# W2 as seven block products, a split last group and a written-out order, in a four-layer graph kernel on one core

## The chip, the cores and the metric

The kernel runs on one core of one Trainium2 chip. The metric is the device time of one execution in microseconds, the median of several runs; lower is better. The engines are named as the profile names them: PE is TensorE (PEld its weight loads), DVE is VectorE, ACT is ScalarE, POOL is GpSimd, SP is SyncE, which here only issues DMAs.

## The reference, cut to what matters

128 graphs of 64 nodes with 256 features pass four layers. After each, the input is added and the sum is normalized over the features. Everything is float32.

```python
# layer 0: five steps of message passing with a GRU
for l in range(5):
    m = h @ weight[l]
    agg = einsum('bij,bid->bjd', A, m)
    h = gru_cell(agg, h, w_ih, w_hh, b_ih, b_hh)
x = layernorm(x + h * nodemask[..., None])
# layer 1: W1 is 256 x 1024, W2 is 1024 x 256
agg = epsilon * x + einsum('bnm,bmd->bnd', adj, x)
h = silu(rmsnorm(agg @ W1 + b1, rms_weight))
x = layernorm(x + h @ W2 + b2)
# layer 2: logmap0, aggregation over adj, expmap0, projection on a ball
x = layernorm(x + project(expmap0(adj @ logmap0(x))))
# layer 3: attention, e_i and f_j from h = x @ W_w.T + W_b
a = adj * exp(e_i + f_j + a_b);  a = a / sum(a)
x = layernorm(x + a @ h)
```

The logarithm in layer 2 is artanh(n)/n. For small n the kernel takes a power series instead of the quotient, and picks by comparing n with `SERIES_BELOW`.

## The kernel before, in words

Two graphs make a block of 128 rows; four blocks make a group of 512 rows (`NB = 4`, `R = 512`, `HR = 256`). There are 16 groups, and `group(g)` writes down all operations of one. Each group is a stream; up to four streams are in work at a time. Buffers are named slots: most tags (`U`, `V`, `agg`, `A`, `B`, `y`, `h`) exist once or twice for each of three slot sets (`s = g % 3`), so a group takes the slots of the group three before it. PSUM has eight banks, handed out one by one.

The GRU (`gated`, called five times) multiplies weights of 256 rows by activations of 256 rows as a two-by-two block product with seven products in place of eight (`gate`, L817, for the two gates; `prod`, L823, for the new state). Sums of activation blocks come from VectorE (`sums`, by way of `summing`, L354); sums of weight blocks are made once (`sums_of`, L445). W1 is done in the same way (`by_sums`, L1000). W2 is plain in the kernel before: for each half h of a group, two blocks of 128 rows, each the sum of eight matmuls with 256 columns, accumulated in a bank `ps_o1` (L316 is the helper line `matmul`). `onto_rows` (L707) then adds the bank to the residual `xb` on VectorE, and for all groups but the last two lets the same instruction give the row sums (`accum_out`) for the normalization.

`layer_norm` takes the mean from these row sums and the variance from a ScalarE square with accumulation (L725); the last two groups use VectorE's statistics instead (L733, L734). Powers of -0.5 and the like are GpSimd instructions (L737). Small scalars per row (`tiny`) have a small tile each. In layer 2 the small arithmetic runs on GpSimd for most groups (`few`, `few_s`), on VectorE for the last two. Layer 3 takes the attention weight `wattP`, whose rows are permuted to fit the transposed x3 that a DMA delivers; the last two groups transpose on TensorE (`feats_of`, L668) and use `wattT`. ScalarE's functions lie in several tables; changing from one to another is a table load. The clock of TensorE is granted by a throttle, and is shown in the profile.

The order of the operations on each engine is not that of the code. `Plan.advance` simulates engines with given durations and, in stretches of 7 us, ranks the ready operations in one of four ways, which the string `CHOICES` picks for each stretch. `Flow.issue` emits the operations in the resulting order and adds dependencies that pin the order on each engine. Some operations have two possible engines (`either`, `copied`, `scaled`), and the plan chooses.

The seven products in `gate` and `by_sums` use the scheme whose weight sums are set up like this, before any group:

```python
for o, x0, x1, op in ((ms1, ms4, mn22, OP.add), (ms3, m11, ms4, OP.subtract), (ms2, ms1, m11, OP.subtract), (ms4, m12, ms2, OP.subtract)):
    dve(512, lambda o=o, x0=x0, x1=x1, op=op: nc.vector.tensor_tensor(
        w1f[:, o, :], w1f[:, x0, :], w1f[:, x1, :], op), [(w1f, o)], [(w1f, x0), (w1f, x1)])
```

Of the kernel before, what the change touches and what calls it, by code (L numbers as in the profile page):

```python
# [22 lines left out]
SERIES_BELOW = 0.25  # L23
# [19 lines left out]
class Op:  # L43
    __slots__ = ("eng", "us", "run", "ways", "stream", "n", "kb", "sets", "need", "then", "bufs", "opens", "id", "way", "port")

    def __init__(self, ways, stream, n, kb, sets, port=()):
        self.port = port
        self.ways = {eng: (us, run) for eng, us, run in ways}
        self.eng, self.us, self.run = ways[0]
        self.stream, self.n, self.kb, self.sets = stream, n, kb, sets  # L50
        self.need, self.then, self.bufs, self.opens, self.id, self.way = 0, [], (), None, 0, 0.0


class Plan:


    def __init__(self, flow):
        self.flow = flow
        ops = [o for s in flow.streams for o in s]
        self.need = [o.need for o in ops]  # L60
        self.at = [0.0] * len(ops)
        self.uses = {}
        self.clock = dict.fromkeys(flow.AHEAD, 2.5)
        self.queues = [{e: deque(o for o in s if e in o.ways) for e in self.clock} for s in flow.streams]
        self.banks = [0.0] * BANKS
        self.left, self.first, self.bus = len(ops), 0, 0.0
        self.lands = [0.0] * flow.TRANSFERS
        self.order, self.table, self.port = [], None, 0.0

    def advance(self, until, rank):  # L70


        flow, need, at, clock, banks = self.flow, self.need, self.at, self.clock, self.banks
        while self.left and clock["PE"] < until:
            best = None
            for s in range(self.first, min(self.first + flow.WINDOW, len(self.queues))):
                for e, q in self.queues[s].items():
                    opened = False
                    for _, o in zip(range(flow.AHEAD[e]), q):
                        t = max(clock[e], at[o.id], self.port) if e in o.port else max(clock[e], at[o.id])  # L80
                        if o.opens is not None:
                            if opened or not banks or need[o.id]:
                                opened = True
                                continue
                            t = max(t, banks[0])
                        elif need[o.id]:
                            continue
                        elif o.kb and e != "POOL":
                            t = max(t, self.lands[0])
                        elif o.sets and self.table not in o.sets:  # L90
                            t += flow.TABLE
                        key = (t + flow.SOONER if len(o.ways) > 1 and e == "DVE" else t, *rank(s, o))
                        if best is None or key < best[0]:
                            best = key, o, e, t
            if best is None:
                return False
            _, o, eng, t = best
            if o.sets and self.table not in o.sets:
                self.table = o.sets[0]
            for e in o.ways:  # L100
                self.queues[o.stream][e].remove(o)
            self.order.append((eng, o))
            end = t + o.ways[eng][0]
            clock[eng] = end
            if eng in o.port:
                self.port = end
            if o.opens is not None:
                banks.pop(0)
            for b in o.bufs:
                n = self.uses.get(b, b.left) - 1  # L110
                self.uses[b] = n
                if not n:
                    banks.append(end + flow.hop(eng, "PE"))
                    banks.sort()
            if o.kb:
                self.bus = max(self.bus, end + flow.DMA[0]) + o.kb / flow.DMA[1]
                end = self.bus + flow.DMA[2]
                if o.eng != "POOL":
                    self.lands = [*self.lands[1:], end]
            for u in o.then:  # L120
                need[u.id] -= 1
                at[u.id] = max(at[u.id], end + flow.hop(eng, u.eng))
            self.left -= 1
            while self.first < len(self.queues) and not any(self.queues[self.first].values()):
                self.first += 1
        return True


class Flow:

    AHEAD = {"PE": 32, "DVE": 10, "ACT": 10, "POOL": 4, "SP": 2}


    HOPS = {"from PE": 0.22, "to PE": 0.42, "else": 0.06, "own": 0.0}

    REACH = {"from PE": 0.22, "to PE": 0.15, "else": 0.06, "own": 0.0}

    SOONER = 0.4


    DMA = (2.0, 330.0, 1.0)
    TRANSFERS = 8
# [89 lines left out]
def kernel(  # L242
# [392 lines left out]
    def group(g):  # L635
# [76 lines left out]
        def layer_norm(y, st, tag, name, norm=None):  # L712
# [6 lines left out]
            def row(b):  # L719
                return [(y, b)]  # L720
# [529 lines left out]
```

## Time and profile before

| What | Value |
|---|---|
| median of 3 runs | 2296.64 us (2296.31 to 2298.32) |
| the profiled execution, its own time | 2296.92 us |
| its span, first to last instruction | 2295.1 us |
| mean granted TensorE clock | 0.994 of full speed |
| instructions | 32440 |
| busy: PE, DVE, ACT, POOL | 2245.7, 1696.8, 1308.8, 554.3 us |

The page gives busy time by engine, then the span in 40 slices, DMA queues, the chain of work that ended last and the costliest groups of instructions. In a group's line the part after the bar is the group's busy time and the mean duration of one instruction, then the idle time of the engine just before them and what ended it. A matmul of float32 data shows as two records of the same shape, each with a weight load. Matmuls are pipelined, so that their durations overlap; how fast they follow one another is read from their starts in the timeline. The stretches (windows) give the same busy times for chosen parts of the span.

### The profile page before, as it was taken

The numbers are of one execution on the slowest core, as the hardware profiler recorded it, in microseconds if no ns is written. First come the engines' busy times: TensorE is split into PE (matmuls) and PEld (weight loads), VectorE is DVE, ScalarE is ACT, GpSimd is POOL, SyncE is SP. The second block draws the span as 40 slices with busy tenths as digits, with TensorE's granted clock in tenths as the row PEclk, the third lists the DMA queues.
The fourth block names the chain that finished last, engine by engine and source line by source line (L and its number), as shares of the span: only waits on it lengthen the run. The fifth ranks groups of instructions, "written<-read, shape, count | busy, mean of one in ns | idle before, by whom it ended". The sixth has DMA issues, their size and how long they took to land.

```text
span 2295.1 us, 32440 instructions
## 1 busy us (share of the span) xinstructions
PE 2245.7 (98%) x11242; PEld 1979.1 (86%) x11242; DVE 1696.8 (74%) x3633; ACT 1308.8 (57%) x2800; POOL 554.3 (24%) x902
## 2 busy tenths in 40 slices
PE   9999999999999999999999999999999999999986
PEld 7888888888888888888888888888888888888774
DVE  5777867767777778677777777778777777777776
ACT  3344656675556556566566656556565665555564
POOL 2200222441122223132322223222231322112201
PEclk9999999999999999999999999999999999999998
DMA  5111112121212012121211212012122121211200
GB/s 146 33 23 33 28 19 58 19 49 29 48 28 47 22 28 58 19 45 33 36 42 25 52 28 47 21 29 49 28 49 37 22 53 21 49 19 20 46 10 19
DMA packets 428771, 84.21 MB, mean 37 GB/s; under 512 B 399124, under 2 KB 427824, under 8 KB 428608
## 3 DMA queue, kind: packets, MB, share of 16 engines
q1 hardware_dynamic: 426880, 80.26, 17.7%
q8 instruction: 89, 1.46, 0.3%
q10 hardware_dynamic: 1328, 1.31, 0.2%
q0 software_dynamic: 400, 0.57, 0.1%
q14 instruction: 74, 0.61, 0.1%
HBM read 32.55 MB, written 8.39 MB: 18 GB/s over the span
## 4 chain that ended last, share of the span: by engine, by line
PE 93%; DVE 3%; ACT 1%; POOL 1%; DMA 1%; issue 1%; SPq 0%; POOLq 0%; ACTq 0%; DVEq 0%
PE p_ga L817 23%; PE p_gc L817 12%; PE ps_o L316 9%; PE ps_agg L316 7%; PE p_ix L823 6%; PE p_gb L817 6%; PE p_hx L823 6%; PE p_ah L1000 4%; PE p_hy L823 4%; PE p_iy L823 4%; PE ps_a L316 2%; PE p_ch L1000 2%; PE ps_att L316 1%; PE ps_sup L316 1%; PE p_bh L1000 1%; PE ps_wmih L316 1%
## 5 line engine op out<-in xcount | busy, mean ns | idle before, releaser
L316 PE MATMUL ps_o<-w2s,hid 128*128 128x256 f32 x1024 | 230.9, 379 | 4.3 <-ACT hid L1051 4.3
L316 PEld LDWEIGHTS ps_o<-w2s,hid 128*128 128x128 f32 x1024 | 194.0, 190 | 31.7 <-ACT hid L1051 5.5
L351 POOL TENSOR_SCALAR mv<-st 128x4 f32<-128x4 f32 x56 | 15.6, 278 | 829.5 <-DVE y L707 442.0
L339 ACT ACTIVATE hnb<-p_hx,half_b 128x256 f32<-128x256 f32 x213 | 100.3, 471 | 143.0 <-PE p_hx L823 111.7
L817 PE MATMUL p_gc<-tA,w_h 128*128 128x256 f32 x640 | 173.2, 381 | 0.1
L817 PE MATMUL p_gc<-tB,w_a 128*128 128x256 f32 x640 | 172.3, 379 | 1.1 <-DVE tB L354 1.0
L817 PE MATMUL p_ga<-tA,w_h 128*128 128x256 f32 x640 | 171.7, 379 | 0.0
L817 PE MATMUL p_ga<-tB,w_a 128*128 128x256 f32 x640 | 168.4, 379 | 1.1 <-DVE tB L354 1.1
L817 PE MATMUL p_ga<-hT,w_h 128*128 128x256 f32 x640 | 168.3, 380 | 0.7 <-DVE U L867 0.4
L817 PE MATMUL p_ga<-agg,w_a 128*128 128x256 f32 x640 | 167.1, 379 | 0.0
L316 PEld LDWEIGHTS ps_agg<-edge,hr 128*128 128x128 f32 x1024 | 142.2, 193 | 12.4 <-DVE a_t L621 3.0
L316 PE MATMUL ps_agg<-edge,hr 128*128 128x128 f32 x1024 | 143.5, 276 | 2.8 <-DVE a_t L621 2.6
L870 ACT ACTIVATE U<-U,half_b 128x512 f32<-128x512 f32 (+1 forms) x160 | 94.0, 628 | 79.7 <-DVE U L867 79.6
L817 PEld LDWEIGHTS p_gc<-tB,w_a 128*128 128x128 f32 x640 | 121.0, 190 | 17.8 <-DVE tB L354 1.6
L817 PEld LDWEIGHTS p_ga<-tB,w_a 128*128 128x128 f32 x640 | 120.5, 190 | 18.1 <-DVE tB L354 1.8
L817 PEld LDWEIGHTS p_gc<-tA,w_h 128*128 128x128 f32 x640 | 121.2, 191 | 16.6 <-ACT V L334 0.5
L817 PEld LDWEIGHTS p_ga<-agg,w_a 128*128 128x128 f32 x640 | 119.7, 190 | 15.7 <-issue 0.5
L817 PEld LDWEIGHTS p_ga<-hT,w_h 128*128 128x128 f32 x640 | 118.5, 190 | 16.0 <-DVE U L867 0.8
L817 PEld LDWEIGHTS p_ga<-tA,w_h 128*128 128x128 f32 x640 | 117.9, 190 | 14.1
L334 ACT COPY agg<-ps_agg 128x512 f32<-128x512 f32 x140 | 81.0, 579 | 78.9 <-PE ps_agg L316 77.9
L870 ACT ACTIVATE V<-V,half_b 128x256 f32<-128x256 f32 (+1 forms) x160 | 87.8, 586 | 59.5 <-DVE V L867 58.9
L883 DVE TENSOR_TENSOR V<-p_ix,V 128x256 f32<-128x256 f32 x192 | 80.6, 420 | 35.3 <-PE p_ix L823 32.4
(285 smaller groups left out, 5667.1 us busy)
## 6 DMA issues: line engine op xcount, KB each, us to landing
hr<-t SPq DMA_DIRECT2D x256, 128.0 KB, 3.2
x<-in_x_dram SPq DMA_DIRECT2D x64, 128.0 KB, 2.7
xr<-in_x_dram SPq DMA_DIRECT2D x16, 512.0 KB, 4.3
out_dram<-x_n SPq DMA_DIRECT2D x16, 512.0 KB, 2.9
xs<-in_x_dram SPq DMA_DIRECT2D x120, 64.0 KB, 2.4
x3T<-t SPq DMA_DIRECT2D x56, 128.0 KB, 3.1
edge<-in_adj_dram SPq DMA_DIRECT2D x64, 32.0 KB, 2.2
wm<-in_L_gnn_weight_dram SPq DMA_DIRECT2D x5, 256.0 KB, 3.3
```

Of the source, the lines that this page charges most:

```text
L316: return nc.tensor.matmul(o, lhsT, rhs, start=(k == 0), stop=(k == nk - 1))
L334: flow.either([("ACT", 0.22 + 0.00077 * n, lambda: nc.scalar.copy(o(), i())), ("DVE", 0.145 + 0.00105 * n, lambda: nc.vector.tensor_copy(o ...
L339: flow.either([("ACT", 0.3 + 0.0008 * n, lambda: nc.scalar.activation(o(), i(), AF.Identity, bias=bias(), scale=scale())), ("DVE", 0.145 + ...
L351: pool(0.25, lambda: nc.gpsimd.tensor_scalar(w[0](), x(), s0, s1, op0, *((op1,) if op1 else ())), [w[1]], r)
L817: pe(HR, lambda i=i, w=w, c=c: nc.tensor.matmul(ps[:, c * HR:(c + 1) * HR], w[:, m, c * P:(c + 1) * P], v[i][0](), start=first and i == 1 ...
L823: pe(HR, lambda: nc.tensor.matmul(ps[:, j * HR:(j + 1) * HR], w[:, m, :], v[0](), start=first, stop=True, skip_group_check=True), [ps], [( ...
L870: act(HR if len(w) == 1 else R, lambda: nc.scalar.activation(o(), src(), AF.Tanh, bias=half_b[:, i * KD + c:i * KD + c + 1], scale=0.5), w ...
L883: dve(HR + 44, lambda: nc.vector.tensor_add(uu[:, c, half(n)], region(ps, j), uu[:, c, half(n)]), [(uu, (n, c))], [ps, (uu, (n, c))])
L1000: pe(HR, lambda c=c: nc.tensor.matmul(ps[:, c * HR:(c + 1) * HR], w1f[:, w, (2 * q + c) * P:(2 * q + c + 1) * P], v[0](), start=first and ...
```

## The change

1. W2 is held as seven blocks of 512 x 128 (`w2f`), four of them loaded and four combinations made on GpSimd (`w2_less`), in place of the plain `w2s`. In groups 0 to 14, `by_sums_back` multiplies the hidden activations by W2 as a two-by-two block product with seven products of eight matmuls, each with 128 columns. VectorE makes eight sums of activation blocks of 128x512 (`sums`) and seven additions from PSUM to the residual (`onto`). Two banks are held, `p_ox` and `p_oy`. The row sums come from an additional ScalarE pass in `layer_norm`.
2. Group 15 keeps plain sums for W2, as matmuls of 128 columns. To get the missing block back, one combination is undone.
3. Group 15's layers 2 and 3 are two streams of two blocks each. They take slot sets of their own, load ScalarE's tables ahead of use (`table`), and in the second piece put small transposes of no use to the output on TensorE (`busy`).
4. The order is no longer planned: each step of the emission is a mark in the string `ORDER`, which names the stream, engine and place in that engine's waiting list (`placed`).
5. The series of layer 2 has three terms fewer, with `SERIES_BELOW` at 0.125 in place of 0.25. The small scalars share one tile for each slot set (`FEW`). The plain attention weight lives in a work slot at the start and is brought back by DMA for the last two groups (`att_plain`). Silu takes the hidden chunks in the order 0, 1, 4, 5, 2, 3, 6, 7.

```diff
-SERIES_BELOW = 0.25
+SERIES_BELOW = 0.125
...
-class Plan:
...
+    def placed(self):
+        at, n = self.SIGNS.index, len(self.SIGNS)
+        waiting = [{e: [o for o in s if e in o.ways] for e in self.ENGINES} for s in self.streams]
+        first, marks = 0, iter(self.ORDER)
+        for c in marks:
+            i = at(next(marks)) * n + at(next(marks)) if c == "~" else at(c)
+            i, e = divmod(i, len(self.ENGINES))
+            i, s = divmod(i, self.AHEAD)
+            o, eng = waiting[first + s][self.ENGINES[e]][i], self.ENGINES[e]
...
-    w2s = fixed([P, KH, D], "w2s")
...
+    w2f = fixed([P, 7, KQ, P], "w2f")
...
+    for o, k, n in ((w11, 0, 0), (w21, 1, 0), (w22, 1, 1), (wd3, 0, 1)):
+        flow.op("SP", 0.6, lambda o=o, k=k, n=n: nc.sync.dma_start(w2f[:, o], w2k[k, n]), [(w2f, o)], kb=256)
+    for o, x0, x1 in ((wd1, wd3, w11), (wd2, w22, wd1), (wd3, w22, wd3), (wd4, w21, wd2)):
+        w2_less(o, x0, x1)
+    wattT = unit("A", S, "wattT", (P, KD, D + 2))
...
+            if summed and of:
+                for b in range(NB):
+                    act(400, lambda b=b: nc.scalar.activation(
+                        o[:, b, :], y[:, b, :], AF.Identity, accum_out=st[:, b, 0:1]), [(o, b), (st, (0, b))], row(b))
...
+                def sums(q):
+                    for o, x0, x1, op in ((s1, a21, a22, OP.add), (s2, s1, a11, OP.subtract), (a21, a11, a21, OP.subtract), (s4, a12, s2, OP.subtract)):
+                        summing(R, lambda o=o: val(o[q]), lambda x0=x0: val(x0[q]), lambda x1=x1: val(x1[q]), op,
+                                o[q][1], [*x0[q][1], *x1[q][1]])
...
+                prod(px, 0, w11, a11, True)
+                prod(py, 0, w21, a12, True)
+                onto(0, 0, px, 0)
+                prod(py, 1, wd3, a21)
+                onto(0, 0, py, 0)
+                prod(px, 0, wd2, s2)
+                onto(1, 1, py, 1)
+                onto(1, 0, px, 0)
+                prod(py, 1, wd4, a22)
+                prod(px, 0, wd1, s1)
+                onto(1, 0, py, 1)
+                onto(1, 1, px, 0)
+                prod(px, 0, w22, s4)
+                onto(0, 1, px, 0)
...
+            if g == NG - 1:
+                w2_less(wd3, w22, wd3)
...
+        def busy(after, n=6):
+            if piece and base:
+                ps = bank("ps_warm")
...
     for g in range(NG):
         flow.stream()
-        group(g)
+        made = group(g)
+        for i in range(2 if made else 0):
+            flow.stream()
+            group(g, ((g + 1 - i) % NF, SIZES[g] // 2, SIZES[g] // 2 * i, *made))
```

## The prediction

> **What bounds the kernel now.** I read the page first: TensorE is busy for 98% of the span and carries 93% of the chain that ended last. The question is therefore how long its list of matmuls is, and where it stands idle.
>
> ```profile
> PE 2245.7 (98%) x11242; PEld 1979.1 (86%) x11242; DVE 1696.8 (74%) x3633; ACT 1308.8 (57%) x2800; POOL 554.3 (24%) x902
> PE 93%; DVE 3%; ACT 1%; POOL 1%; DMA 1%; issue 1%; SPq 0%; POOLq 0%; ACTq 0%; DVEq 0%
> ```
>
> Second, the stretches (columns: us, then busy us and instructions of PE, PEld, DVE, ACT and POOL, granted clock, DMA share, GB/s).
>
> ```profile
> 1000.00:1500.00 500.00, 499.48 (x2529) 443.97 (x2528) 374.33 (x792) 302.51 (x649) 128.79 (x202) 1.00 0.19 38
> 1500.00:2000.00 500.00, 499.39 (x2518) 443.25 (x2518) 375.91 (x802) 294.05 (x649) 135.33 (x231) 1.00 0.19 38
> 2150.00:2200.00 50.00, 41.39 (x197) 35.12 (x194) 39.04 (x96) 24.20 (x51) 5.25 (x7) 0.93 0.13 33
> 2200.00:2250.00 50.00, 45.92 (x220) 39.76 (x221) 33.48 (x75) 27.50 (x45) 6.95 (x5) 0.97 0.00 1
> 2250.00:2270.00 20.00, 8.44 (x29) 5.93 (x28) 14.66 (x71) 12.32 (x35) 4.62 (x4) 0.83 0.00 0
> 2270.00:2296.00 26.00, 14.12 (x62) 11.17 (x61) 16.02 (x60) 13.08 (x31) 3.87 (x3) 0.76 0.12 40
> ```
>
> In the middle TensorE lacks 1.1 us of 1000, and VectorE is at 75%. Of its 49.4 us idle in all (2295.1 - 2245.7), some 36 lie after 2150, at a lower clock besides. Third, the timeline of TensorE gives the true price of a matmul; the mean durations (379 ns) overlap, so starts are compared.
>
> ```profile
> 1015.61 0.59 PE L823 MATMUL p_hx<-tA,w_hn 128*128 128x256 f32 x2
> 1016.04 0.59 PE L823 MATMUL p_hy<-tA,w_hn 128*128 128x256 f32 x2
> 1016.48 1.05 PE L316 MATMUL ps_agg<-edge,hr 128*128 128x128 f32 x8
> 1017.37 0.38 PE L678 MATMUL ps_hr<-ident,hT 128*128 128x128 f32 x2
> ```
>
> A matmul with 256 columns appears as two records, 0.432 us from start to start (1015.61 to 1016.04 to 1016.48), 0.216 a record. With 128 columns and fresh weights each time, eight records take 0.89 us: 0.111 each, 0.2225 a matmul. So half the width costs 1.03 of half the time. Last, the groups and the chain at the end.
>
> ```profile
> L316 PE MATMUL ps_o<-w2s,hid 128*128 128x256 f32 x1024 | 230.9, 379 | 4.3 <-ACT hid L1051 4.3
> L707 DVE SCALAR_TENSOR_TENSOR xb<-ps_o,xb 128x256 f32<-128x256 f32 x64 | 24.9, 420 | 27.6 <-PE ps_o L316 27.6
> L357 POOL TENSOR_TENSOR sqt<-sqt,sqh 128x512 f32<-128x512 f32 x56 | 73.0, 1304 | 127.2 <-ACT sqh L986 124.0
> ```
>
> ```profile
> 2230.05 22.03 PE ps_o L316 x102
> 2252.11 0.76 DVE xb L707 x2
> ...
> 2254.28 1.65 POOL rstd L737
> ```
>
> The W2 of groups 14 and 15 is the last dense work; from 2252.1 to 2295.1, 43.0 us, both groups go through layers 2 and 3 side by side.
>
> **What the Trainium skill says.** "TensorE: Matmul & The Clock Gate", section "Wait — 56ns, not 53.3ns?", gives N / 2.4 GHz plus 2.5 ns for a warm matmul. A record here passes its columns twice by its price: 512 / 2.4 + 2.5 = 215.8 ns and 256 / 2.4 + 2.5 = 109.2; the trace has 216 and 111, so narrow matmuls are nearly free of overhead. The same page, "What's actually happening", has the clock halve after an idle window of some 3.4 us; the trace agrees, with granted clocks of 0.83 and 0.76 in the last two stretches. "SBUF — State Buffer", section "Who interferes with whom", lets a VectorE instruction with two SBUF inputs exclude a GpSimd one that reads SBUF: all eight new sums per group are of that kind. In this trace POOL's sqt sums stretch from a median of 1274 ns to at most 1761, which fits and doesn't prove it.
>
> **The change, part by part.**
>
> *W2 in seven products, groups 0 to 14.* Removed per group: 64 records of 256 columns, 64 x 0.2158 = 13.81 us. Added: 7 products of 8 matmuls, 112 records of 128 columns, 112 x 0.1112 = 12.45. Fifteen times 1.36 is 20.3. Group 15 stays plain but narrow: 128 x 0.1112 = 14.23, 0.4 worse. Net -19.9 us. Bounds for the narrow price, as no run of over 16 narrow records is shown: the skill's 109.2 ns (1808 records: -23.6), and 125, midway to the 140 that the group of ps_agg gives by its busy time (143.5 / 1024, the tails of short runs in it): +5.0. I take 111.2, since that spacing was measured with a weight load for every record.
>
> *What feeds them.* VectorE per group: 8 sums of 128x512 from SBUF, 0.70 each (L354 shows 0.69 to 0.75), 5.6; 7 adds from PSUM of 256 elements, 0.42 (L883), 2.9; gone are 4 adds with accumulator, 4 x (0.42 + 0.08) = 2.0. So +6.5 us, and the instruction list moves some 1.5 more of copies and scalings from ScalarE to it. ScalarE: 4 passes for the row sums, 0.50 + 0.19 each, +2.8. A group takes 138 us (W2 starts at 810.3 and 948.2), so VectorE goes from 75 to about 80%, ScalarE from 60 to 61%. I cost this at nothing: other groups' gates lie on TensorE meanwhile. Without that cover a group would expose the 5.6 of sums ahead of the products, and four waits in p_ox (each product after the first needs its bank read, 0.42 or 0.84 plus about 0.3 of hops): 8 to 9 us. Behind the sums on VectorE stand the gates' adds from PSUM, for which TensorE waits; the trace has VectorE at 80% and more in single stretches with TensorE full, so I allow +2 over all, bounds 0 and +10.
>
> *Setup and small steps.* Four weight loads of 256 KB for two of 512, four POOL subtractions at about 1.3 (the sqt row, same size). W2 is first wanted at 292 us, but the subtractions stand on POOL ahead of the sums for layer 1's weights (w_a), which group 0's gates want; the table of waits has POOL idle 39.1 us there for ScalarE's w_a, so their 5.2 fit. If the loads, put on SP among the other weights, come late, w_a waits with them: a few us once. The plain attention weight now comes by four DMAs of 64 KB in group 13, on SP ahead of nothing that is due for 100 us; its place in slot A is returned before group 2 wants it, or costs some us once. The shorter series drops 6 POOL operations of 0.29 in 14 groups (24 us of an engine at 24%: nothing now) and 3 of 0.17 on VectorE for each chain at the end.
>
> *The end.* After the last W2 matmul I follow the list for two-block pieces with the durations of the rows at the end of before. Adds, statistics, power: 3.2 us, but VectorE is in the first piece's scalar chain till 5.3; second piece's chain, 14 x 0.17, 7.7; scaling, aggregation, two squares, 10.1; power, tanh, two ball chains of 6 x 0.18, 14.0; y and statistics 16.1; power, offset, two scalings 18.5; transposes and copies 20; attention of the one piece and of the other, 24.5; final sums, statistics, two queued powers and the last scaling 30.8; store 4.4. About 35 against 43.0, bounds 31 and 40. What is late next is the other piece's attention, and group 14's last normalization, which is put behind both. The 24 filling transposes cost nothing where TensorE is idle; they hold the clock, which cost some 5 us here (20.5 busy for 15.6 of work at 0.216).
> TensorE's work after the last W2 shrinks from 15.6 to 13.9 (group 14's aggregation goes ahead of it): that 1.7 is added to the time before.
>
> *The order.* Groups 14 and 15 no longer do W2 together: between group 15's W1 and W2 only group 14's aggregation (1.7) covers a chain of copy 0.6, two squares 1.4, sum 0.7, row sums 0.8, power 1.3, ps_rms 0.6, VectorE 0.74, Silu 0.7 and 0.6 of hops, 7.4 in all: some 5.7 idle where before lost about 3.5, +2.2. Against this stand the waits that TensorE has now (table of waits: us in total, times, longest):
>
> ```profile
> PE p_hy L823 <- DVE y L707: 3.7, 1, 3.7
> PE p_ah L1000 <- ACT hid L334: 3.0, 3, 1.4
> PE p_ah L1000 <- DVE hid L1005: 2.7, 1, 2.7
> ```
>
> With 1.2 (ps_hr behind y L707) and 4.3 (ps_o behind hid, in the groups above) they are 14.9. An order set one operation at a time can put other products there; I take half, -7.5, bounds 0 and -14. With the +2 of VectorE: about -3.3, bounds -14 and +8.
>
> Sum on the profiled execution: span 2295.1 - 19.9 + 1.7 - 8.0 - 3.3 = 2265.6; I keep 1.4 in hand for the reordered start and call it 2267. With the 1.8 around the span that is 2268.7 against 2296.92, and the median stood 0.3 lower: 2268.
>
> **Rivals.**
> 1. *The end doesn't shorten.* Group 15's pieces share VectorE, and one's chain delays the other's; the cover lost ahead of W2 is not regained. For it: by my list some 14 of the end's first 20 us are VectorE or its waits for POOL. Then 2296.6 - 19.9 + 1.7 - 1 = 2277.
> 2. *The order removes nearly all avoidable waits.* Pre-tail idle falls by 14 and the end to 31: 2296.6 - 19.9 + 1.7 - 12 - 14 = 2252. Against it: VectorE has less slack than before.
> 3. *VectorE takes TensorE's place in W2.* p_ox is a chain of four products with a VectorE read between; if neighbouring gates wait in VectorE's queue behind the 5.6 of sums, every group stalls. Full exposure, 8.5 x 15 = 127 less the 28 above, gives about 2395; the side turns at (19.9 + 8) / 15 = 1.9 us per group. Half a group's sums exposed, 2.8: 2311. Against it: 1.1 us idle in 1000 with VectorE at 75%, and up to three other groups' products in the list between.
> That the change doesn't do what it says is excluded for W2: the instruction list has the 840 and 64 narrow matmuls.
>
> **How the numbers follow.** Forecast 0.62, rival 1 0.19, rival 2 0.14, rival 3 0.05. The range 2254 to 2281 takes the forecast's bounds and rival 1, and leaves out most of rivals 2 and 3. A difference under 0.2% (4.6 us) can't be told from no change: faster 0.95, within 0.02, slower 0.03.
>
> **What would show it.** p_ox and p_oy together 1680 records, spaced 0.111; TensorE's busy time near 2222; VectorE near 1810; idle in 1000 to 2000 still under 5; from the last ps_o to the end about 35, with a clock nearer 0.9. Spacing of 0.12 or more, or waits of p_ox on VectorE above 2 us a group, would prove me wrong.

## The result, and the profile after

| | Before | After | Forecast |
|---|---|---|---|
| median of 5 runs each, us | 2296.64 (2296.31 to 2298.45) | 2289.12 (2286.62 to 2291.02) | 2268 (2254 to 2281) |
| profiled execution, its own time / span, us | 2296.92 / 2295.1 | 2286.62 / 2284.8 | 2268.7 / 2267 |
| busy PE, us | 2245.7 | 2237.4 | near 2222 |
| busy DVE, us | 1696.8 | 1827.1 | near 1810 |
| TensorE idle, 1000 to 2000 us | 1.1 | 8.6 | under 5 |
| last matmul of W2 to the end, us | 43.0 | 36.0 | about 35 |

The ratio is 0.9963, 95% interval [0.9949, 0.9978]: faster, clear of the scatter, but by 7.5 us where 28.6 were forecast. The time lies 8 us above the upper end of the range. The profiled execution is the fastest of the five; the accounts by trace below are of it, and its span is 10.3 us shorter than that of before.

The page of after, busy time and the chain that ended last by engine:

```profile
PE 2237.4 (98%) x12050; PEld 1982.7 (87%) x12050; DVE 1827.1 (80%) x3832; ACT 1307.4 (57%) x2856; POOL 536.7 (23%) x827
PE 89%; DVE 6%; DMA 1%; ACT 1%; SPq 1%; issue 1%; POOL 0%; ACTq 0%; DVEq 0%; POOLq 0%
```

TensorE has 808 records more and is busy for less time. VectorE is at 80%, as forecast. But VectorE's share of the chain of work that ended last has gone from 3% to 6%, and TensorE's from 93% to 89%: the way back from the end now leads through VectorE more often.

The stretches of after (us, then busy us and instructions of PE, PEld, DVE, ACT and POOL, granted clock, DMA share, GB/s):

```profile
1000.00:1500.00 500.00, 494.90 (x2671) 441.91 (x2670) 407.16 (x833) 300.43 (x656) 124.45 (x187) 1.00 0.21 37
1500.00:2000.00 500.00, 496.50 (x2707) 444.14 (x2706) 410.96 (x837) 296.43 (x669) 127.95 (x208) 1.00 0.22 37
2150.00:2200.00 50.00, 45.17 (x268) 39.19 (x267) 44.84 (x86) 31.16 (x65) 12.35 (x20) 1.00 0.19 33
2200.00:2250.00 50.00, 41.66 (x252) 36.34 (x251) 37.13 (x115) 34.45 (x73) 10.68 (x11) 0.93 0.03 11
2250.00:2270.00 20.00, 15.78 (x72) 11.85 (x72) 16.79 (x84) 12.69 (x40) 4.13 (x5) 0.91 0.00 0
2270.00:2285.00 15.00, 4.19 (x17) 2.53 (x16) 8.08 (x36) 5.87 (x14) 2.40 (x3) 0.76 0.21 71
```

In the middle TensorE is idle for 5.1 and 3.5 us of 500 each, where before had 0.5 and 0.6. That is where the forecast is most clearly missed. The end, from the last matmul of W2, looks as it said: 36 us in place of 43 at a higher clock. In the order before, after:

```profile
2252.10:2295.10 43.00, 20.49 (x80) 15.62 (x80) 28.96 (x121) 24.02 (x63) 8.49 (x7) 0.79 0.07 25
2248.80:2284.80 36.00, 21.02 (x98) 15.18 (x96) 25.83 (x121) 19.73 (x55) 6.53 (x8) 0.86 0.09 30
```

The groups of W2 in after:

```profile
L1173 PE MATMUL p_oy<-w2f,hid 128*128 128x128 f32 x720 | 98.2, 275 | 1.3 <-DVE hid L434 1.1
L1173 PE MATMUL p_ox<-w2f,s 128*128 128x128 f32 x720 | 98.0, 275 | 0.5 <-DVE s L434 0.3
L1173 PE MATMUL p_ox<-w2f,hid 128*128 128x128 f32 x240 | 35.2, 275 | 0.0
L1182 DVE TENSOR_TENSOR xb<-p_ox,xb 128x256 f32<-128x256 f32 x60 | 25.2, 420 | 9.8 <-PE p_ox L1173 8.7
L396 PE MATMUL ps_o<-w2f,hid 128*128 128x128 f32 x128 | 17.1, 302 | 1.6 <-ACT hid L1149 1.6
```

The new products are all there (1680 records), and TensorE stood idle just before them for 1.8 us in the whole program. W2 itself runs as it was meant to. What is lost must lie ahead of other work.

To find it I took every matmul's distance to the start of the next one, less its price (0.216 us for 256 columns, 0.111 for 128, what undisturbed records of the traces take), and summed what is left by stretch. This is waiting and slow clock together, and it counts waits too short to be seen as idle time:

| Stretch, us | Before | After | After with GpSimd's sums in quarters (below) |
|---|---|---|---|
| 0 to 400 | 9.3 | 7.6 | 8.7 |
| 400 to 600 | 3.5 | 10.4 | 10.7 |
| 600 to 1000 | 2.5 | 1.3 | 2.5 |
| 1000 to 2000 | 2.2 | 13.5 | 4.4 |
| 2000 to 2150 | 1.9 | 0.6 | 0.7 |
| 2150 to the last matmul | 36.1 | 29.5 | 28.1 |
| sum | 55.4 | 63.1 | 55.0 |
| price of all matmuls | 2225.9 | 2208.8 | 2208.8 |

The price falls by 17.1 us: 19.8 from W2, less 2.7 for the 24 filling transposes. The waits rise by 7.7. The difference is the 10.3 us of the span, with under 1 us from what follows the last matmul. A change of the narrow price by 0.4 ns moves the two sums of after by 1.5 us against each other, and the middle stretch by 0.6.

**What stands in the way at 1017 us.** The timeline of after, four lines of it (start us, us, engine, line, operation; in brackets the idle time before it and what ended it):

```profile
1014.08 0.68 DVE L1040 SCALAR_TENSOR_TENSOR hT<-hT,V 128x512 f32<-128x512 f32 x1
...
1017.49 2.61 POOL L437 TENSOR_TENSOR x_n<-x_n,wb_r 128x1024 f32<-128x1024 f32 x1 [8.16 <-DVE t L1355]
...
1017.92 2.73 DVE L1040 SCALAR_TENSOR_TENSOR hT<-hT,V 128x512 f32<-128x512 f32 x1
...
1020.80 0.63 PE L771 MATMUL ps_hr<-ident,hT 128*128 128x128 f32 x4 [0.87 <-DVE hT L1040]
```

The same VectorE instruction takes 0.68 us at 1014.08 and 2.73 at 1017.92. The second starts 0.43 us after a GpSimd sum of two operands, which ends at 1020.10, and it ends 0.55 us after that. It did next to nothing while GpSimd ran. Then TensorE waits for its result. The Trainium skill ("SBUF — State Buffer", section "Who interferes with whom") says that a VectorE instruction with two SBUF inputs contends with a GpSimd instruction that reads SBUF, because its second input comes through an interface that both share, and "Issue order, not op shape, decides who blocks"; these four lines agree, with 2.73 us for 0.68. Below, and in the expectations, "the port" is this shared interface.

In after, 52 VectorE instructions take over 0.15 us more than is usual for their kind, 46.1 us in all (before: 36, and 28.4 us). 24.1 us of it lie beside GpSimd's `sqt` sums, 9.5 beside this `x_n` sum of 128x1024 and 9.4 beside `xb<-x_n,b_r`. These sums aren't new: before has them too.

That this is a block and not a general slowdown shows in how the 52 end. 49 of them begin while a GpSimd operation runs and end at a fixed distance behind its end: 0.55 us for two inputs of 128x512 (26), 0.28 to 0.29 for two inputs of 128x256 (14) and for a comparison of 128x512 with one input (`edge`, 5), 0.02 for 128x2 (4). So two SBUF inputs aren't the only case. 112 VectorE additions that take one operand from PSUM begin during GpSimd sums too, and none of them is longer than usual by more than 0.01 us. GpSimd's powers, mostly of 128x4 and some 1.04 us each, don't block either, an exception that the skill's rule doesn't make: 40 VectorE instructions with two SBUF inputs begin during one, and none is longer by more than 0.02 us.

What TensorE waits for in the middle of after, 1000 to 2000 us (us in total, times, longest; before has three waits there, 1.2 us in all):

```profile
PE ps_att L396 <- DVE y L800: 2.0, 2, 1.1
PE p_bh L1098 <- DVE aggm L415: 1.0, 1, 1.0
PE p_ga L915 <- DVE U L965: 0.9, 1, 0.9
PE ps_hr L771 <- DVE hT L1040: 0.9, 1, 0.9
PE p_hx L921 <- DVE hnb L420: 0.7, 1, 0.7
PE p_ga L915 <- DVE tB L434: 0.6, 1, 0.6
```

The six longest are all for VectorE and make 6.1 of the 8.6 us. Six of the seven waits in these lines end within 1.5 us of the end of a stretched VectorE instruction; the exception is `p_hx`. `ps_att` and `p_bh` follow instructions held up by the `xb` sum, `ps_hr` and `p_ga` others held up by `x_n` and `sqt`.

### The profile page after: what moved, and what is told of

The parts are those of the page before. It is cut to its first block, busy times and chain, and to the rows that moved or that the text cites. A ratio compares the mean times of both kernels' runs of the same rounds, so it can differ in the third digit from the quotient of the medians.

```text
span 2284.8 us, 34210 instructions
## 1 busy us (share of the span) xinstructions
PE 2237.4 (98%) x12050; PEld 1982.7 (87%) x12050; DVE 1827.1 (80%) x3832; ACT 1307.4 (57%) x2856; POOL 536.7 (23%) x827
## 3 DMA queue, kind: packets, MB, share of 16 engines
q1 hardware_dynamic: 428144, 80.52, 19.9%
## 4 chain that ended last, share of the span: by engine, by line
PE 89%; DVE 6%; DMA 1%; ACT 1%; SPq 1%; issue 1%; POOL 0%; ACTq 0%; DVEq 0%; POOLq 0%
PE p_ga L915 23%; PE p_gc L915 11%; PE ps_agg L396 7%; PE p_ix L921 6%; PE p_gb L915 6%; PE p_hx L921 6%; PE p_iy L921 5%; PE p_ox L1173 4%; PE p_hy L921 4%; PE p_ah L1098 4%; PE p_oy L1173 3%; PE ps_a L396 2%; PE p_ch L1098 2%; PE ps_sup L396 1%; PE ps_att L396 1%; PE p_bh L1098 1%
## 5 line engine op out<-in xcount | busy, mean ns | idle before, releaser
L915 PE MATMUL p_ga<-hT,w_h 128*128 128x256 f32 x640 | 177.4, 380 | 0.9 <-DVE U L965 0.9
L419 ACT ACTIVATE hnb<-p_hx,half_b 128x256 f32<-128x256 f32 x202 | 95.1, 472 | 105.7 <-PE p_hx L921 82.5
L396 PE MATMUL ps_agg<-edge,hr 128*128 128x128 f32 x1024 | 150.6, 276 | 4.3 <-DMA hr<-t 2.8
L915 PEld LDWEIGHTS p_ga<-tB,w_a 128*128 128x128 f32 x640 | 120.1, 190 | 16.9 <-DVE tB L434 1.3
L915 PEld LDWEIGHTS p_gc<-tB,w_a 128*128 128x128 f32 x640 | 119.7, 190 | 16.9 <-DVE tB L434 1.2
L915 PEld LDWEIGHTS p_ga<-tA,w_h 128*128 128x128 f32 x640 | 117.5, 190 | 14.2
L834 POOL TENSOR_TENSOR rstd<-ve,pow 128x4 f32<-128x4 f32 (+2 forms) x67 | 80.2, 1197 | 136.2 <-DVE ve L832 124.8
L822 ACT ACTIVATE x_n<-y,mv 128x256 f32<-128x256 f32 x168 | 83.4, 499 | 38.4 <-POOL mv L431 38.4
```

The lines of the kernel that those rows point to most:

```text
L396: return nc.tensor.matmul(o, lhsT, rhs, start=(k == 0), stop=(k == nk - 1))
L419: flow.either([("ACT", 0.3 + 0.0008 * n, lambda: nc.scalar.activation(o(), i(), AF.Identity, bias=bias(), scale=scale())), ("DVE", 0.145 + ...
L822: act(400, lambda b=b: nc.scalar.activation(o[:, b, :], y[:, at + b, :], AF.Square, bias=mv[:, b, 0:1], accum_out=st[:, b, 1:2]), [(o, b), ...
L834: pool(1.25, lambda: nc.gpsimd.tensor_tensor(rstd[:, :m, :], ve[:, :m, :], pow2[:, :m, :NB], OP.pow), [rstd], [ve])
L915: pe(HR, lambda i=i, w=w, c=c: nc.tensor.matmul(ps[:, c * HR:(c + 1) * HR], w[:, m, c * P:(c + 1) * P], v[i][0](), start=first and i == 1 ...
```

## The experiments

All ratios are against the kernel before, on the same chip. Theories go by letters in the expectations: A, the first, is that the new sums load VectorE too heavily; D, formed after the first four runs, is that GpSimd's sums block VectorE. What another theory holds is said where it is tested.

**1. The new sums cut to one column.**

```diff
-   summing(R, lambda o=o: val(o[q]), lambda x0=x0: val(x0[q]), ...
+   summing(R, lambda o=o: val(o[q])[:, :, :1], lambda x0=x0: val(x0[q])[:, :, :1], ...
```

> The changed kernel, but each of VectorE's eight sums per group ahead of the seven products works on one column of 256 instead of all, and the three products that take a sum of their own tile take the identity instead (part of W2's product is left out; the matmuls keep number, shape and order). Theory A, VectorE's new load is what TensorE waits for in the middle: the changed kernel's waits from 400 to 2000 us (by start-to-start spacing 25 us over the price of the matmuls, 8 before) fall to about 10, VectorE goes from 80% to 76 or 77%, time 2271 to 2277. Theory B, the written order causes the waits whatever VectorE's load: 2286 to 2291.

Measured: 2289.38 us (2287.84 to 2290.33), 0.9962 [0.9948, 0.9975]; VectorE's busy time falls by 61 us to 1765.9. TensorE's idle time from 1000 to 2000 is 9.0 us (after: 8.6). Theory A falls for the sums: they were taken away, and the time didn't move. The 61 us are not all of VectorE's new load, which is 130 us; the seven additions and the work moved from ScalarE stay in this run, and no run takes them away.

**2. The same sums made twice.** (The first is made three times and the third, which overwrites its own input, once: twice the number in all.)

```diff
+   def run(..., times={id(s1): 3, id(a21): 1}.get(id(o), 2)):
+       return [nc.vector.tensor_tensor(val(o[q]), val(x0[q]), val(x1[q]), op) for _ in range(times)]
```

> The changed kernel with every one of the eight sums per group issued twice over (same result), VectorE near 84%. Theory A: waits grow faster than the load, TensorE's idle time in the middle by 20 us or more, time 2310 or above. Theory B: at most 2295, since the sums have slack.

Measured: 2356.18 us, 1.0251 [1.0237, 1.0265]. Idle from 1000 to 2000 is 31.7 us. The page of this run, the chain by engine:

```profile
PE 78%; DVE 15%; ACT 2%; DMA 2%; issue 1%; SPq 1%; POOL 0%; DVEq 0%; ACTq 0%; POOLq 0%
```

So the slack that hides the sums ends between one and two times their number: VectorE's 80.5 us more (1907.6 against 1827.1) cost 67 us. The sums are free as they are, and most of a second set is exposed. The run lengthens the chain ahead of the products and adds load to VectorE at once; it doesn't tell the two apart.

**3. One of the four sums on GpSimd.**

```diff
+   if o is s4:
+       flow.op("DVE", 0.7, lambda ...: ("POOL", nc.gpsimd.tensor_tensor(val(o[q]), val(x0[q]), val(x1[q]), op)), ...)
```

> The changed kernel with the last sum (s4, two of the eight per group, wanted by the last product only) on GpSimd at about 1.3 us each instead of VectorE at 0.7. Theory A: 21 us off VectorE, a quarter of the sums, gives 3 to 6 us: 2283 to 2286. Theory B: within 2 us of 2289. A loss above 2 us would mean that GpSimd's sums hold up VectorE's two-input instructions.

Measured: 2290.52 us (2289.52 to 2293.6), 0.997 [0.9959, 0.9981]. No gain. VectorE's stretched instructions rise from 46.1 to 59.4 us, 13 to 15 of them beside the moved sums. The loss of 1.4 us against after is below the 2 us that I had set as the sign, so the time proves nothing; the stretched instructions pointed to theory D: work moved to GpSimd comes back as blocked VectorE.

**4. Filling transposes in group 15, between W1 and W2.**

```diff
+   def filled(ps, n, first, run): ...
+       return [*(nc.tensor.transpose(ps[:, P:2 * P], ident.tile(), ident.tile()) for _ in range(n)), run()]
```

> The changed kernel with 12, 10 and 12 transposes of no use to the output put on TensorE in group 15 just ahead of the row sums, of the transposes of the scale and of the first W2 matmul, where TensorE waits 1.6, 1.4 and 1.6 us. If the lower clock there is what makes group 15's W2 take 16.9 us for 14.2 of work, W2 falls to 14.5 and the time by 2 to 3 us, to 2286; the waits in the middle stay as they are in both theories. If the clock isn't the reason, 2289.

Measured: 2290.87 us (2287.08 to 2292.01), 0.9965 [0.9953, 0.9978]. Nothing is gained. But the run doesn't do all that was planned. TensorE has 22 records more, 12 ahead of the row sums and 10 ahead of the transposes of the scale; the 12 ahead of the first W2 matmul are missing, because the test on the loop variable `h` is evaluated after its loop has ended, when `h` is 1 and no longer 0. The wait there is as long as in after:

```profile
2236.71 0.49 PE L396 MATMUL ps_o<-w2f,hid 128*128 128x128 f32 x2 [1.59 <-ACT hid L1154]
2237.37 15.86 PE L396 MATMUL ps_o<-w2f,hid 128*128 128x128 f32 x126 [0.17 <-ACT hid L1154]
```

W2 of group 15 takes 16.4 us in place of 16.9, but it does so in runs 3 and 5 as well, which have no fill. The granted clock was 0.53 from 2223 to 2230 and 0.57 from 2237 to 2241. So the run doesn't settle whether a filled gap would keep the clock up in W2.

**5. GpSimd's sums of `sqt` and `x_n` cut to one column.**

```diff
-   pool_sum(NB * D, lambda: x3.tile(), lambda: x3.tile(), ...)
+   pool_sum(NB * D, lambda: x3[:, 0, :1], lambda: x3[:, 0, :1], lambda: wb_r[:, :1], ...)
```

> The changed kernel, but GpSimd's sums of the squares (sqt) and its sum of x3 and the bias (x_n) in groups 0 to 13 work on one column (these sums are left out of the result); the order is the same. In the changed kernel 40 VectorE instructions with two SBUF inputs last 0.5 us or more over their usual time, 46 us in all against 28 before, nearly all beside such a GpSimd sum, and 10 of TensorE's waits from 1000 to 2200 us follow one of them within 2 to 5 us. Theory D, the written order sets GpSimd's long sums beside VectorE's and TensorE waits for what VectorE then delivers late: the long ones fall to under 15 us, TensorE's waits from 1000 to 2200 (22 us over the price of the matmuls) halve, time 2275 to 2280. Theory B, TensorE's place in the order is too early by itself: 2286 to 2291.

Measured: 2280.47 us (2279.35 to 2282.46), 0.9927 [0.9913, 0.994]: 8.7 us below after, and 9.6 below run 8, which is after itself beside this run. Stretched VectorE instructions fall to 12.2 us, and idle from 1000 to 2000 to 5.1. The sum `xb<-x_n,b_r` is whole in this run, and of the waits listed above those behind it stay, while `ps_hr` and both of `p_ga` are gone:

```profile
PE ps_att L396 <- DVE y L800: 1.9, 2, 1.1
PE p_bh L1101 <- DVE aggm L415: 1.0, 1, 1.0
```

That supports D, though results of GpSimd that come earlier could have helped too. Run 6 excludes that.

**6. GpSimd's sums of `sqt`, `x_n` and `xb` whole, but each in four instructions.** Nothing of the computation is left out.

```diff
+   def split_sum(n, o, x0, x1, w, r):
+       pool(0.24 + 0.00211 * n, lambda: [nc.gpsimd.tensor_tensor(a, b, c, OP.add) for a, b, c in zip(o(), x0(), x1())], w, r)
-   pool_sum(NB * D, lambda: xb.tile(), lambda: x1.tile(), lambda: over(b2_r.tile(), NB), ...)
+   split_sum(NB * D, lambda: [xb[:, b, :] for b in range(NB)], ..., lambda: [b2_r.tile()] * NB, ...)
```

> The changed kernel with each of GpSimd's sums of 128x512 and 128x1024 as four instructions of a quarter (same result, GpSimd some 20 to 40 us busier). Theory D, if VectorE gets in between two pieces: a delay is then 0.4 to 0.6 us instead of up to 2.4, and the time falls by 4 to 8 us, to 2281 to 2285. If the pieces follow one another without VectorE getting in, nothing is won: 2289. Theory B: 2289.

Measured: 2278.70 us (2277.34 to 2279.76), 0.9917 [0.9904, 0.9931]. This is faster than both kernels, by some 18 us against before, 10.4 against after and 11.4 against run 8. The middle of this run, and the waits of TensorE that the profile lists there:

```profile
1000.00:1500.00 500.00, 499.51 (x2712) 448.10 (x2711) 402.44 (x843) 301.58 (x659) 149.90 (x300) 1.00 0.21 37
1500.00:2000.00 500.00, 499.03 (x2714) 447.26 (x2714) 401.62 (x838) 301.83 (x677) 149.43 (x304) 1.00 0.22 39
...
PE ps_agg L396 <- DMA hr<-t: 0.6, 1, 0.6
PE ps_a L396 <- DMA x3T<-t: 0.2, 1, 0.2
PE p_hx L924 <- DVE hnb L420: 0.2, 1, 0.2
PE p_ga L918 <- DVE tB L434: 0.2, 1, 0.2
```

TensorE is idle for 1.5 us of 1000 with the same new W2, the same order and VectorE still at 80% there; the waits for VectorE have fallen to 0.4 us, and `ps_att` and `p_bh` are gone too. Stretched VectorE instructions are down to 18.3 us. The instruction from above, in the timeline of this run:

```profile
1018.81 4.46 POOL L440 TENSOR_TENSOR x_n<-x_n,wb_r 128x256 f32<-128x256 f32 x4 [6.96 <-DVE t L1361]
...
1020.44 1.10 DVE L1043 SCALAR_TENSOR_TENSOR hT<-hT,V 128x512 f32<-128x512 f32 x1
...
1021.30 0.47 PEld L774 LDWEIGHTS ps_hr<-ident,hT 128*128 128x128 f32 x3
```

VectorE gets in between two quarters after some 0.4 us and is done in 1.10. GpSimd pays: the four take 4.46 us in place of 2.61. GpSimd as a whole is busy for 75 us more, at 27%, which costs little in this order: from 400 to 600 us TensorE waits 1.2 us for `sqt`, which it doesn't in after. As GpSimd's own results come later here and not earlier, the gain must come from VectorE.

**7. Without the 24 filling transposes of the end.**

```diff
-   turn(lambda i=i: nc.tensor.transpose(ps[:, i % 4 * P:(i % 4 + 1) * P], after.tile()[:, :1].to_broadcast([P, P]), ident.tile()), ...)
+   turn(lambda: [], [ps], [after])
```

> The changed kernel without the 24 filling transposes in the last group's second piece. The prediction has them hold TensorE's clock at the end: without them the clock of the last 25 us falls below the 0.79 that it has now, and the time rises by 1 to 3 us. If the clock falls anyway, the time stays at 2289 or falls by some tenths.

Measured: 2291.18 us (2290.0 to 2292.25), 0.9972 [0.9961, 0.9983]. The time is 1 to 2 us longer, which the intervals don't tell from none. The traces do: from the last matmul of W2 to the end this run takes 37.5 us, and the nine profiled executions with the fill (after, and runs 1, 3 to 6, 8 and 9) take 36.0 to 36.2. The granted clock over that stretch is 0.80 here and 0.86 in both profiles of after:

```profile
2252.90:2290.50 37.60, 20.09 (x74) 13.53 (x73) 25.95 (x121) 19.87 (x55) 6.53 (x8) 0.80 0.08 28
```

So the fill is worth 1.5 us, by one execution without it.

**8. After once more, for its scatter.**

> The changed kernel itself once more, beside these. All theories: 2289 again, within 2286 to 2292, with its waits in the same places to some tenths of a microsecond, since its order is fixed.

Measured: 2290.09 us (2286.94 to 2292.03), 0.9966 [0.9955, 0.9978]. Most of TensorE's waits in the middle come back at the same operations with the same sizes (`ps_att` 2.0 us, `p_bh` 1.0, `ps_hr` 0.9, `p_ga` 0.9 and 0.6); `p_hx` behind `hnb` goes from 0.7 to 1.0, and `ps_a` behind its DMA from 0.5 to 0.9.

**9. Quarters and fill together, and quarters without the sums.**

> The changed kernel with GpSimd's sums in quarters (2278.7 us by itself), and with 11 and 13 filling transposes of no use to the output ahead of the scale's transposes and of the first W2 matmul in group 15, where TensorE waits 1.4 and 1.6 us. In the kernel with quarters the clock is halved twice here, for 6.8 us each, the second time from the row sums into W2, which takes 16.9 us for 14.2 of work. If the waits' idle time decides the second drop: W2 in 14.5 to 15, time 2276 to 2277. If the activity before (the waits in W1) decides it, as the earlier run with fillers hints: 2278 to 2280.

Measured: 2278.41 us (2276.05 to 2280.29), 0.9918 [0.9905, 0.9932], the time of run 6. W2 of group 15 takes 17.1 us. Here too the fill ahead of the first W2 matmul is missing: TensorE has 11 records more, not 24, and waits 1.59 us there. The 11 ahead of the scale's transposes win nothing.

> The changed kernel with GpSimd's sums in quarters, and VectorE's eight sums per group on one column, with the identity in place of three of them (part of the product left out, as before). With the delays by GpSimd gone, is VectorE's new load the next to cost? If so: 2270 to 2274. If the sums have slack, as without the quarters: 2277 to 2280.

Measured: 2279.59 us (2279.02 to 2279.96), 0.9924 [0.9909, 0.9939]. With most of the port's delays gone, the new sums still cost nothing: VectorE at 77 or 79% makes no difference.

**10. Quarters in the kernel before.** The edit is that of run 6, in the old kernel.

> The kernel before, with its own order and GpSimd's sums in quarters. It has 28 us of stretched VectorE instructions, but only some 12 us of TensorE's waits from 300 to 2100 us. If the delays by GpSimd cost there as well: 2292 to 2294. If the old order had put them where nothing waits for them: 2296 to 2298, so that the quarters pay in the written order alone.

Measured: 2296.80 us (2293.48 to 2298.71), 0.9995 [0.9987, 1.0003]. Stretched instructions fall from 28.4 to 20.3 us, and nothing is won: idle from 1000 to 2000 was 1.1 us and is 0.8. So 8 us less of blocked VectorE are worth nothing in this order. That blocking costs only where TensorE soon needs the blocked result fits this and run 6, but isn't shown by a run of its own.

**11. Only narrow matmuls in the kernel before.** Part of W2's sums isn't kept in its output.

```diff
-   ps[:, j * D:(j + 1) * D], chunk(k)[0][:, b * P:(b + 1) * P], w2s[:, k, :], k, KH)
+   ps[:, j * D + n * P:j * D + (n + 1) * P], chunk(k)[0][:, b * P:(b + 1) * P], w2s[:, k, n * P:(n + 1) * P], ...) for n in range(2)]
```

> The kernel before, with each W2 matmul of 256 columns as two of 128 (same products, same order). It measures the price of narrow matmuls in long runs: at 111 ns a record 1024 of 216 become 2048 of 111, 6.9 us more less what waits take up, 2302 to 2304. At 125 ns a record it would be 2320 or more.

Measured: 2307.11 us (2304.81 to 2307.59), 1.0042 [1.0028, 1.0056]: 9.3 us more. Its group:

```profile
L1059 PE MATMUL ps_o<-w2s,hid 128*128 128x128 f32 x2048 | 240.1, 277 | 4.2 <-ACT hid L1051 4.2
```

Starts are 0.112 us apart in this run, over 2048 narrow records. 2048 x 0.112 less 1024 x 0.216 is 8.2 us; the price of 0.111 gives 6.1, and the interval reaches from 6.4 to 12.9. The half-width price of the forecast holds on long rows of narrow matmuls, or is 1% too low. By the time alone it could lie from 0.1111 to 0.1143.

**12. A planned order for the new operations.** Three runs have all of after's operations, but the order comes from a plan like that of the kernel before, with choices found anew. In the first the plan keeps VectorE's and GpSimd's instructions of two SBUF inputs apart; in the second it doesn't know of that; the third is the second with the quarters of run 6.

```diff
-                        t = max(clock[e], at[o.id], self.port) if e in o.port else max(clock[e], at[o.id])
+                        t = max(clock[e], at[o.id])
```

> The operations of after, every one, in an order planned as in the kernel before (the plan keeps VectorE's and GpSimd's instructions with two SBUF inputs apart), with choices found anew for these operations. If the written-out order is what meets the blocked port, TensorE is idle for under 3 us of the 1000 between 1000 and 2000 (after: 8.6, before: 1.1). If any order of these operations meets it with VectorE at 80%, 7 us or more. Between 400 and 600, idle 3 us or less says that the written-out order is at fault there too (after: 6.4), 6 or more that the operations themselves can't be fed in that stretch. The end isn't laid out by hand here, so that it is longer than in after by some 5 to 10 us, and the time tells less than the stretches: 2280 to 2292 us with the first theory, 2290 to 2300 with the second.

> As the planned kernel, but the plan knows nothing of the port that VectorE and GpSimd share, and its choices were found in the same manner without it. If ignorance of the port is what makes an order meet these waits, VectorE's instructions are stretched by 30 us or more in all and TensorE is idle for 6 to 12 us between 1000 and 2000, as in after; the time is 5 to 12 us over that of the planned kernel. The rival, that the written-out order is at fault for another reason, expects the idle time of the planned kernel, and a time within 3 us of it.

> The order planned without the port, and GpSimd's sums in quarters, which leave VectorE gaps to get in. If the port is what counts, the idle time between 1000 and 2000 falls to under 3 us and the time to within 3 us of the planned kernel's or below it. The rival expects no change against the run without quarters, as quarters brought none to the kernel before.

| Run | Median, us | Ratio | Idle 400 to 600 | Idle 1000 to 2000 | VectorE stretched, us |
|---|---|---|---|---|---|
| planned, port known | 2307.73 (2306.17 to 2309.78) | 1.0044 [1.003, 1.0058] | 4.8 | 11.8 | 54.7 |
| planned, port unknown | 2322.58 (2321.41 to 2325.02) | 1.011 [1.0096, 1.0124] | 7.9 | 7.2 | 61.5 |
| the latter in quarters | 2323.82 (2320.84 to 2326.41) | 1.0114 [1.01, 1.0128] | 7.5 | 7.9 | 25.3 |
| after | 2289.12 | 0.9963 [0.9949, 0.9978] | 6.4 | 8.6 | 46.1 |

Most of what I expected here was wrong. A plan that knows of the port still meets it: its VectorE instructions are stretched by 54.7 us, more than in after. Its middle, from the stretches of that run, is worse than that of the written-out order:

```profile
1000.00:2000.00 1000.00, 988.20 (x5356) 882.30 (x5355) 793.94 (x1608) 610.33 (x1357) 251.57 (x388) 1.00 0.21 36
```

Quarters more than halve the stretches in the planned order and win nothing (2323.82 against 2322.58). The waits in the middle say why, first without quarters, then with them:

```profile
PE ps_ss L316 <- POOL sqt L357: 1.3, 3, 0.7
...
PE ps_ss L316 <- POOL sqt L360: 4.3, 5, 1.5
```

TensorE's waits for VectorE fall from 3.1 to 0.5 us, but it now waits for GpSimd's sums themselves, which the quarters make slower.

The first plan is 15 us faster than the second, but not in the middle: the second is idle 4.6 us less there, and longer between 400 and 1000 (15.4 us against 7.4). As the choices of the two plans differ too, the 15 us can't be put down to the port. So it isn't shown that the written-out order is at fault for ignoring the port. What is shown is narrower: in the middle of that order, which leaves TensorE little other waiting, GpSimd's whole sums are what is left. The first plan in quarters wasn't run, though 4.4 us of its waits there are for `hT`. That an order with VectorE at 80% can keep TensorE fed is shown by run 6 alone.

## Why the prediction was wrong, step by step

*W2 in seven products: right.* Forecast -19.9 us, measured -19.8 by number and spacing of the matmuls (0.111 to 0.112). 1680 records are there, and TensorE hardly waits for them. Run 11 agrees with the price. That the scheme saves what it should is shown.

*What feeds them: right for the sums, too small for their neighbours.* The forecast put VectorE at about 80% and the feeding at nothing, with +2 and bounds of 0 and +10 kept for delays of neighbouring work. Runs 1 and 9 show that the sums are hidden, and run 2 that the cover ends before they are doubled. The +2 is counted under the order, below. Rival 3 named the wrong mechanism: TensorE idles 1.8 us ahead of all of W2's products, not 1.9 us in each group.

*The end: right.* Forecast 35, measured 36.0 from the last matmul of W2 to the end. The clock over this stretch was 0.86, where before had 0.79 and the forecast said nearer 0.9; the filling transposes, which were said to hold it, do so and are worth 1.5 us (run 7).

*The order: this step failed.* It was put at -3.3 us, made of -7.5 (half of TensorE's 14.9 us of waits avoided), +2.2 (lost cover ahead of group 15's W2) and +2 (VectorE). From the steps that held, the last matmul of W2 should have ended at 2252.1 - 19.9 + 1.7 = 2233.9 us without it. It ended at 2248.8: where -3.3 was forecast, about +15 was measured. The term that failed most is the +2 for what a busier VectorE delays: it stands for +11.3, beyond its upper bound, because GpSimd's whole sums hold up VectorE instructions that TensorE waits for. By stretch, after less before:

- 1000 to 2000: +11.3, against the +2 that I allowed. This is the largest term, and where it comes from is settled by runs 5 and 6: two different edits of GpSimd's sums take 8.7 and 10.4 us off the time, and the quarters take 9.1 off this stretch. Why the same sums cost nothing in before, the new order or the rest of VectorE's new load, is not settled (run 12). I had named the skill's rule on the port and looked at GpSimd's side only (1274 ns stretched to 1761), and for the eight new sums only. The instructions that are blocked are mostly the GRU's old ones (`hT` 11.7 us of the 46.1, the activation sums `tA` 11.6 and `tB` 7.4), and the blocked engine is VectorE. "I cost this at nothing" was true of the sums and untrue of their neighbours: the cover that I named, other groups' gates, was itself late.
- 400 to 600: +6.9. Not explained. Quarters (10.7) leave it, as does leaving out W2's sums besides (TensorE idle 7.1 us), and no planned order of these operations brought the idle time there to before's 2.7 us; the best has 4.8. VectorE is at 79% there. The waits are several small ones, the longest behind different engines; 2.2 of the 6.4 us of idle time are for the DMA of `hr`, whose median time to landing is 3.8 us in after and 3.2 in before. I didn't follow that up.
- 2150 to 2250: +1.4, where -7.5 + 2.2 = -5.3 was forecast. From 2150 to 2226 waits fell by 6.8 us, as hoped, though `ps_hr` at 2193.6 waits 2.7 us behind an `hT` that the `x_n` sum holds up (2.71 us in place of 0.69; in run 6 this wait is 1.1 us). But the gap ahead of group 15's W2 came on top:

```profile
2222.73 1.13 PE L1098 MATMUL p_ah<-aggm,w1f 128*128 128x256 f32 x4 [0.78 <-DVE hid L1103]
2223.70 1.89 PE L396 MATMUL ps_sup<-tan,adjT 128*128 128x256 f32 x8
2227.19 1.05 PE L396 MATMUL ps_ss<-ones,sqt 128*128 128x1 f32 x8 [1.61 <-DVE sqt L434]
2229.61 0.69 PE L1143 MATMUL ps_rms<-ident,few 128*128 128x128 f32 x4 [1.37 <-POOL few L1140]
2231.89 17.08 PE L396 MATMUL ps_o<-w2f,hid 128*128 128x128 f32 x128 [1.60 <-ACT hid L1149]
2248.81 1.04 PE L761 MATMUL ps_T<-ident,x_n 128*128 128x128 f32 x8
```

This is TensorE's timeline in after. Only `ps_sup` lies between W1 and W2, as I had read from the instruction list, and the three waits make 4.6 us against my 5.7. What I left out is the price afterwards: W2 itself takes 16.92 us (2231.89 to 2248.81) for 128 x 0.111 = 14.2 of work, with the granted clock down: 1.00 from 2220 to 2230, 0.51 from 2230 to 2237. The prediction took the clock to halve after an idle window of some 3.4 us; here it was halved, and the longest wait in the 10 us ahead was 1.61 us. Run 4 filled the first two of the three waits and run 9 the second, and nothing was won; the third, just ahead of W2, was never filled.
- The other stretches up to 2150 make -4.2, of which the start, for which I kept +1.4, is -1.7.

The sum is -19.9 + 1.7 + 15 - 7 = -10.2, against 10.3 measured in the span. As the 15 is what the other steps leave over, this had to come out; the stretches, summed by themselves, give 15.4. None of the rivals describes this: the nearest in time, rival 1, needs an end that doesn't shorten, and the end did.

*What would show it.* TensorE's idle time in the middle (8.6, not under 5) missed and points to the step that failed. Its busy time (2237.4, not 2222) missed too, but is no sign of that step: run 6, without the waits, has 2238.3. A record lasts longer than its distance to the next, so that waits shorter than the difference count as busy.

What stays open: the waits at 400 to 600 us, the slow clock in group 15's W2, what VectorE's additions and moved work cost, and whether an order exists that keeps the whole GpSimd sums out of VectorE's way.

## What to carry to other kernels

An engine's average load says little about the work that another engine waits for: look in the timeline for single instructions that take longer than others of their kind, and at what runs beside them. Where GpSimd and VectorE both add two SBUF operands, try GpSimd's long sums in pieces: it costs GpSimd time, and bounds how long VectorE is held up. That was worth 10 us here, nothing in the kernel before, and in a planned order it only moved the wait from VectorE to GpSimd; so look first at whom TensorE waits for. When a step is costed at nothing because something covers it, ask whether the cover itself can come late.

## What the runs showed of the hardware that I had not expected

- A VectorE sum of 0.68 us took 2.73 us when it began 0.43 us behind a GpSimd sum of 128x1024; with the GpSimd sum in quarters, 1.10 us.
- A held-up VectorE instruction ends at a fixed distance behind the GpSimd one: 0.55 us for two inputs of 128x512, 0.28 to 0.29 for 128x256, in 40 of after's 52. A one-input comparison of 128x512 is held up as well (0.28 to 0.29, 5 times); 112 additions with one operand in PSUM are not, to within 0.01 us, and GpSimd's powers hold up none of 40 two-input instructions.
- Four GpSimd sums of 128x256 took 4.46 us in sequence beside VectorE's work, one of 128x1024 2.61: GpSimd loses by the pieces, and VectorE gains.
- A plan that keeps the two apart on paper doesn't do so on the chip: 54.7 us of stretched VectorE instructions with it, 61.5 without.
- With a fixed order, most single waits behind VectorE come back in a second execution at the same operation to within 0.1 us; one grew by 0.3 us, and one behind a DMA by 0.4.
- The granted clock was 0.51 over 7 us in which dense work began, behind waits of at most 1.61 us each.
